# GpSimd's side work in smaller pieces: a re-spacing of the background steps of an attention and mixture-of-experts kernel

## The chip, the cores and the metric

The kernel runs on one core of one Trainium2 chip. The metric is the device time of one execution in microseconds (us), as the median of several runs. The engines are named as in the profile: PE (TensorE matmul), PEld (its weight load), DVE (VectorE), ACT (ScalarE), POOL (GpSimd), SP (SyncE, here an issuer of DMAs).

## The reference

A block of a transformer on 8 sequences of 1024 tokens with 128 features, in float32:

```
x = x + attention(layernorm(x))          # 8 heads of 16
x = x + moe(layernorm(x))                # 8 experts, the best 2 for each token
score = ((q + u) k^T + rel_shift((q + v) p^T)) / sqrt(128),  p = pos_encoding @ Wp
h = gelu(ln(x @ Wr1 + br1)) @ Wr2 + br2  # router; softmax, top 2, weights made to sum to 1
y_e = (x1 * gelu(x2)) @ W2_e + b2_e,     x1, x2 = split(x @ W1_e + b1_e)
```

The relative-position term is computed with rotation tables, so that content and position score come from products of prepared rows (`z`, `kt` and their copies) with no shift.

## The kernel before, in words

**Stages.** Attention of all eight batches comes first (about 40 to 1460 us of the profile), then the experts (to the end). Attention is cut into 32 blocks: batch b, group g of four heads, half qc of the queries (512). A block has 9 slots (`NU`), each one key tile's worth of scores, and each slot two half slots. There are thus 576 half slots of blocks, and some more until the last block has drained. In a half slot PE makes the scores for two heads of the present block (the running maximum needs them, DVE L518/L522) and the scores of an older block, 11 slots behind, again, from which ACT makes the exponentials px (L543). POOL zeroes the masked part of px (`cut`, L547, instructions L553/555/558); two slots later PE sums px times the values (`weigh`, `av` L593).

**Side work.** Everything else is written as Python generators, which run while the program is built and fix the order of each engine's instructions. `aside(h, sparing)` is called once per half slot h and lets each live generator whose time has come emit its next step; they are visited in the order of `due` (a slot number). In a generator, `yield 0` asks for PE: one such step is let out in a half slot, and in the first half of a slot only if it is due or two wait. `yield k` waits k half slots, a plain `yield` the generator's own gap (1 or 2, 3 for some). Each engine then works through its own queue in this order: an instruction that comes earlier in the program stands in front, whether it is urgent or not. The list of side generators is made by `add(slot, due, gap, make, ...)` (L1005 to 1021):

- `prepare(b)` (L345): layer norm of batch b: moments on DVE, reciprocal root on POOL (L226 to 229), the normalised xn in two POOL instructions of 128x1024 (L359, L360), the load of the next batch (SP, L362), PE's transposes xt (L370), and xall plus the output bias (POOL, L374).
- `keys(b, g)` (L381): products pq (L338), DVE's z and kt (L402), for each half of 512 the sum z + zs on POOL (L408, L409), and then sixteen copies between rows on SP's queue (L414, 415, 418, 419) to zu, ku, kl.
- `values(b)`: pv and vt, the transposed values va.
- `band`, `beside`, `close` for each block: the part of the relative position that lies outside; the division by the sum (L613 to 632, with small DMAs through `sm`, `rd`, `rx`); the sum of both groups (POOL, cx add L636); the output product `po`, added to xall (L643).
- `diagonal` (POOL L527, DVE L530): the masked maximum of the diagonal tile; `shifts` (POOL L567 to 571, PE mt L343): the maxima split in three bf16 parts.

**Routes.** After batches 1, 3, 5 and 7 a `route` is started for two batches (due: never). It normalises the rows (POOL L682, L683), multiplies by Wr1 (ph), scales (L728, L729), turns (hT, L734 to 739), applies GELU by hand on POOL and ACT (polynomial L742 to 744, tanh L772, L774, L775), multiplies by wr2h (logits, pl, L750), picks two experts, and at last scatters its rows with 32 indirect DMAs on POOL's queue (xs, L840). `table_a` and `table_b` make the tables of blocks for the experts. Never-due generators may take more steps in one half slot if these emit nothing that needs a gate:

```
more = 0 if h < 2 * (NU * 4 * NB_A) else 1 if h < 2 * total and not sparing else 3 if h >= 2 * total else 0
```

(`2*NU*4*NB_A` is 432, `2*total` is 576.) The last route works beside the experts ("late"). Experts start once the first three routes and their tables have ended and attention is past its last block.

Of the kernel before, what the change touches and what calls it, by code (L numbers as in the profile page):

```python
# [49 lines left out]
P = 128  # L50
# [98 lines left out]
def kernel(ctx: ExitStack, tc: tile.TileContext, a: dict, out: bass.AP):  # L149
# [125 lines left out]
    with ExitStack() as at:  # L275
# [69 lines left out]
        def prepare(b):  # L345

            sl = slice(b * NT, (b + 1) * NT)
            for n in range(b * NT, (b + 1) * NT):
                moments(rk, mv1, xall[:, n, :], n)
                yield  # L350

            eng = nc.gpsimd if b else nc.vector
            yield from rsqrt(eng, rk, r1[:, sl], col(mv1, 1)[:, sl], 1e-10, "p", 1.0 + 1e-5)
            xn = ap1.tile([P, NT, D], F32, name=f"xn{b}", tag="xn")
            if b == 0:
                for n in range(NT):
                    nc.vector.tensor_scalar(xn[:, n, :], xall[:, n, :], mv1[:, n, 0:1], r1[:, n:n + 1], ALU.subtract, ALU.mult)
            else:
                nc.gpsimd.tensor_tensor(xn, xall[:, sl, :], col(mv1, 0)[:, sl].unsqueeze(2).to_broadcast([P, NT, D]), ALU.subtract)  # L359
                nc.gpsimd.tensor_tensor(xn, xn, r1[:, sl].unsqueeze(2).to_broadcast([P, NT, D]), ALU.mult)  # L360
            if 0 < b < NB - 1:
                nc.sync.dma_start(xall[:, (b + 1) * NT:(b + 2) * NT, :], x_v[:, (b + 1) * NT:(b + 2) * NT, :])  # L362
            yield
            yield 2
            xts[b] = xt = ap1.tile([P, S], F32, name=f"xT{b}", tag="xT")
            for hf in range(NQ):
                yield 0
                pt = bank(f"xt{b}_{hf}") if b else scores(4 + hf)
                for n in range(TQ):
                    nc.tensor.transpose(pt[:, n * P:(n + 1) * P], xn[:, hf * TQ + n, :], ident)  # L370
                nc.scalar.activation(xt[:, hf * QB:(hf + 1) * QB], pt, AF.Identity, bias=gb[:, 1:2], scale=gb[:, 0:1])
                yield
            if b:
                nc.gpsimd.tensor_tensor(xall[:, sl, :], xall[:, sl, :], rows_bc[:, DR + NE:].unsqueeze(1).to_broadcast([P, NT, D]), ALU.add)  # L374
            yield

        def spare(name):
# [3 lines left out]
        def keys(b, g, s):  # L381

            u, xt, kl, ku, bs = f"{b}_{g}", xts[b], kls[g], kus[g], bias[g]
            tbs = []
            for hf in range(NQ):
                tb = apk.tile([P, 2, QB], F32, name=f"tb{u}_{hf}", tag="tb")
                nc.sync.dma_start(tb, a["tab"][g][:, :, hf * QB:hf * QB + QB])
                tbs.append(tb)
            yield 8
            z = apk.tile([P, S + 1], F32, name=f"z{u}", tag="z")  # L390
            zu = apk.tile([P, S], F32, name=f"zu{u}", tag="zu")
            kt = ktp.tile([P, S], F32, name=f"kt{u}", tag="kt")
            s.update(zs=(z, zu), ks=(kl, ku))
            nc.vector.memset(z[:, S:S + 1], 0.0)
            yield
            for hf in range(NQ):
                c, tb = slice(hf * QB, hf * QB + QB), tbs[hf]
                for k, t in enumerate((z, kt)):
                    yield 0
                    pq = bank(f"pq{u}_{hf}_{k}") if b + g else scores(2 * hf + k)  # L400
                    across(pq, wc[g][:, k, :], xt[:, c])
                    nc.vector.scalar_tensor_tensor(t[:, c], pq, bs[:, k:k + 1], tb[:, k, :], ALU.add, ALU.mult)  # L402
                    yield
                if b + g == 0:
                    nc.vector.scalar_tensor_tensor(z[:, c], kt[:, c], halfs[:, 1:2], z[:, c], ALU.mult, ALU.add)
                    continue
                zs = spare(f"zs{u}_{hf}")
                nc.gpsimd.tensor_scalar(zs, kt[:, c], halfs[:, 1:2], None, ALU.mult)  # L408
                nc.gpsimd.tensor_tensor(z[:, c], z[:, c], zs, ALU.add)  # L409

            q2 = nc.sync if b + g else nc.scalar
            for j in range(HG):
                r, e = 32 * j, 32 * j + DH
                nc.sync.dma_start(kl[r:e, 0:S], kt[r:e, :])  # L414
                q2.dma_start(zu[r:e, :], z[r:e, 0:S])
            for j in range(HG):
                r, e = 32 * j, 32 * j + DH
                nc.sync.dma_start(zu[e:r + 32, :], z[e:r + 32, 1:S + 1])
                q2.dma_start(ku[r:e, :], kt[r:e, :])
            yield  # L420
# [193 lines left out]
        def close(n):  # L614
# [18 lines left out]
            if g < NG - 1:  # L633
                cxs[b, qc] = cx
                return
            nc.gpsimd.tensor_tensor(cx, cx, cxs.pop((b, qc)), ALU.add)  # L636
            yield 4
            yield 0
# [20 lines left out]
        def route(t0, late):  # L659
# [16 lines left out]
            eng = nc.vector if late else nc.gpsimd  # L676
            yield from rsqrt(eng, rk, r2, col(mv2, 1)[:, sl], 1e-5)

            def rows(q):
                qs = slice(t0 + q[0], t0 + q[-1] + 1)  # L680
                xn = rw[:, q[0]:q[-1] + 1, 0:D]
                nc.gpsimd.tensor_tensor(xn, xall[:, qs, :], col(mv2, 0)[:, qs].unsqueeze(2).to_broadcast(w), ALU.subtract)  # L682
                nc.gpsimd.tensor_tensor(xn, xn, r2[:, q[0]:q[-1] + 1].unsqueeze(2).to_broadcast(w), ALU.mult)  # L683

            hs = small("hs", [nt, DR], u)
            mvh = small("mvh", [nt, 2], u)
# [20 lines left out]
            for i in range(n_q + 2):  # L707
                for k in range(4):
                    if k == 0 and i < n_q:
                        yield 0  # L710
                        turned(quads[i])
                        if i + 2 < n_q:
                            rows(quads[i + 2])
                    if k == 2 and 1 <= i <= n_q:
                        yield 0
                        narrowed(quads[i - 1])
                    if i >= 2:
                        n = quads[i - 2][k]
                        moments(rk2, mvh, hs[:, n, :], n)
                    if k % 2 == 0 or i >= 2:  # L720
                        yield
# [9 lines left out]
            def turned2(q):  # L731
                pt = bank(f"ht{u}_{q[0]}")[0:DR, :]
                for i, n in enumerate(q):
                    nc.tensor.transpose(pt[:, i * P:(i + 1) * P], hs[:, n, :], ident)  # L734
                hTs[q] = hT = rk2.tile([DR, QB], F32, name=f"hT{u}_{q[0]}", tag="hT")
                if late:
                    nc.scalar.activation(hT, pt, AF.Gelu_apprx_tanh, bias=lns[:, 1:2], scale=lns[:, 0:1])
                    return
                nc.scalar.activation(hT, pt, AF.Identity, bias=lns[:, 1:2], scale=lns[:, 0:1])

                ths[q] = th = rk.tile([DR, QB], F32, name=f"th{u}_{q[0]}", tag="th")
                nc.gpsimd.tensor_tensor(th, hT, hT, ALU.mult)  # L742
                nc.gpsimd.tensor_scalar(th, th, 0.044715, 1.0, ALU.mult, ALU.add)
                nc.gpsimd.tensor_tensor(th, th, hT, ALU.mult)

            def logits(q):
                pl = bank(f"pl{u}_{q[0]}")[:, 0:TQ * NE].rearrange("p (n k) -> p n k", k=NE)
# [9 lines left out]
            for i in range(n_q + 1):  # L757
                if i < n_q:
                    yield 0
                    if i + 2 < n_q:  # L760
                        scaled(quads[i + 2])
                    turned2(quads[i])
                yield
                if i > 0:
                    yield 0
                    logits(quads[i - 1])
                yield
                if i < n_q and not late:
                    yield
                    q = quads[i]  # L770
                    th = ths.pop(q)
                    nc.scalar.activation(th, th, AF.Tanh, scale=0.7978845608028654)  # L772
                    yield
                    nc.gpsimd.tensor_scalar(th, th, 1.0, None, ALU.add)  # L774
                    nc.gpsimd.tensor_tensor(hTs[q], th, hTs[q], ALU.mult)  # L775
                    yield


            def over(t):
# [229 lines left out]
        for m, (b, g) in enumerate(groups):  # L1009
            state[b, g] = {}  # L1010
            t0 = 2 * NU * m
            if m > 0:
                if g == 0:
                    add(t0 - 3 * NU + 2, t0 - 9, 1, prepare, b)
                add(t0 - NU - 1, t0 - 2 * NU, 1, keys, b, g, state[b, g])
            if g == 0:
                add(max(t0 - NU + 7, 0), t0 + 6, 1, values, b)
        for n in range(len(blocks_)):
            t0 = NU * n
            add(t0 + 2, t0 + 6, 3, band, n)  # L1020
# [52 lines left out]
        with tc.manual_schedule():  # L1073
# [56 lines left out]
            for t in range(last):  # L1130
# [4 lines left out]
                for half in range(2):  # L1135
# [27 lines left out]
                    if ua and a_units[ua[1]][0] == "dia":  # L1163

                        for i, (j, p) in enumerate(zip(ja, pa_)):
                            up = ap5.tile([P, QB], F32, name=f"up{ua[0]}_{j}", tag="up")
                            between.append(lambda p=p, up=up: nc.scalar.copy(up, p))
                            live.append(dict(due=t + 6, next=2 * t + half + i % 2, gap=1, gate=False,
                                             steps=diagonal(ua[0], j, up.rearrange("p (t c) -> p t c", c=P))))
                    elif ua:  # L1170
                        greatest(*ua, ja, pa_)
# [256 lines left out]
```

## Time and profile before

| what | us |
|---|---|
| median of 3 runs | 1891.94 (1890.9 to 1891.97) |
| the profiled execution | 1936.66 |
| its span, first to last instruction | 1934.8 |
| mean granted TensorE clock in it | 0.961 |
| PE, DVE, POOL, ACT busy | 1801.1, 1211.9, 1018.0, 971.0 |
| first expert matmul h (L1234) | at 1461.45 |

The page gives, beside the busy time of each engine, the span in 40 slices of 48.4 us (a digit is a tenth; PEclk is the granted clock in tenths), the chain that ended last, and groups of instructions by line. The trace can be asked for the waits of one engine ("engine line tile, what it waited for, total, times, longest"), the busy time by windows, and every instruction in order of time. A mark [8.47 <-POOL hT L775] says that the engine stood for 8.47 us before this instruction and what ended that.

Attention takes 74% of the span. In the part behind it (1461 to 1935) PE multiplies the experts' matrices.

### The profile page before, as it was taken

How to read it: one execution, taken by the hardware profiler on the slowest of the kernel's cores; microseconds unless marked ns; L12 is line 12 of the kernel's file. 1: busy time of each engine (PE TensorE's matmuls, PEld its weight loads, DVE VectorE, ACT ScalarE, POOL GpSimd, SP SyncE). 2: the span in 40 equal slices, each digit the busy share in tenths (PEclk: the TensorE clock that was granted, in tenths of full speed). 3: DMA queues.
4: the chain of work that ended last, by engine and by line, in shares of the span. 5: the costliest groups of instructions: out<-in, count | busy, mean ns of one | idle time of the engine just before them, and what ended most of it. 6: DMA issues, size and time to landing. Idle time of an engine off the chain costs nothing. (4 is left out here: it accounts for less than half of the span.)

```text
span 1934.8 us, 44523 instructions
## 1 busy us (share of the span) xinstructions
PE 1801.1 (93%) x16906; PEld 992.3 (51%) x16906; DVE 1211.9 (63%) x3203; ACT 971.0 (50%) x1851; POOL 1018.0 (53%) x1414
## 2 busy tenths in 40 slices
PE   6999999999998999899899999998989998789995
PEld 2344444444443444445344434444436887678885
DVE  5667676687685766677757566767624555444454
ACT  1265655656655555556555546655544443234442
POOL 2154363456448557763774775484752434543354
PEclk8699999999998999999989999999989999899998
DMA  5021010210102011211101120101114455455596
GB/s 153 1 59 26 27 37 28 50 35 29 26 27 37 27 36 53 58 35 30 37 26 28 54 41 27 27 27 26 32 48 142 161 170 179 142 172 188 193 322 195
DMA packets 97287, 145.65 MB, mean 75 GB/s; under 512 B 25345, under 2 KB 68610, under 8 KB 97074
## 3 DMA queue, kind: packets, MB, share of 16 engines
q1 hardware_dynamic: 78448, 117.65, 21.9%
q0 software_dynamic: 8912, 18.15, 2.6%
q10 hardware_dynamic: 9714, 7.02, 1.2%
q8 instruction: 133, 2.18, 0.5%
q14 instruction: 80, 0.66, 0.1%
HBM read 102.17 MB, written 23.55 MB: 65 GB/s over the span
## 5 line engine op out<-in xcount | busy, mean ns | idle before, releaser
L543 ACT ACTIVATE px<-sc 128x512 f32<-128x512 f32 x1152 | 632.9, 597 | 541.5 <-PE sc L507 316.8
L522 DVE CUSTOM_DVE_ANT_0 jk<-sc,wide 128x512 f32<-128x512 f32 x576 | 396.8, 689 | 156.2 <-PE sc L507 112.4
L507 PE MATMUL sc<-kl,z 32*128 32x512 f32 (+3 forms) x1536 | 404.3, 551 | 18.4 <-ACT px L543 12.1
L507 PE MATMUL sc<-ku,zu 32*128 32x128 f32 (+3 forms) x2304 | 376.9, 408 | 12.4 <-ACT px L543 8.5
L518 DVE TENSOR_REDUCE mx<-sc 128x1 f32<-128x512 f32 x448 | 287.8, 684 | 142.4 <-PE sc L507 123.0
L507 PE MATMUL sc<-zu,ku 32*128 32x512 f32 (+3 forms) x1536 | 360.1, 546 | 0.0
L593 PE MATMUL av<-px,va 128*32 128x256 f32 (+3 forms) x3792 | 351.3, 442 | 6.3 <-POOL px L555 6.2
L507 PE MATMUL sc<-z,kl 32*128 32x512 f32 (+3 forms) x1536 | 339.2, 520 | 0.2 <-ACT px L543 0.2
L1263 POOL DMA_INDIRECT ys<-yo,to x142 | 137.1, 966 | 230.6 <-DVE to L1259 79.3
L507 PEld LDWEIGHTS sc<-ku,zu 32*128 32x128 f32 x2304 | 200.6, 191 | 76.0 <-ACT px L543 53.1
L1238 DVE SCALAR_TENSOR_TENSOR gt<-h,wb,gl 128x256 f32<-128x256 f32 x280 | 135.4, 484 | 165.6 <-ACT gl L1237 125.6
L1237 ACT ACTIVATE gl<-h,wb 128x256 f32<-128x256 f32 x280 | 132.2, 473 | 169.3 <-PE h L1235 120.2
L507 PEld LDWEIGHTS sc<-kl,z 32*128 32x128 f32 x1536 | 142.5, 188 | 141.1 <-ACT px L543 100.9
L1234 PE MATMUL h<-xt,wb 128*128 128x256 f32 x560 | 174.0, 393 | 26.8 <-ACT yb L1247 10.4
L593 PEld LDWEIGHTS av<-px,va 128*32 128x32 f32 x3792 | 75.3, 108 | 231.9 <-issue 148.6
L1235 PE MATMUL h<-xt,wb 128*128 128x256 f32 x560 | 171.7, 389 | 0.0
L555 POOL TENSOR_SCALAR_AFFINE_SELECT px<-px 128x516 f32<-128x516 f32 (+1 forms) x128 | 84.8, 663 | 161.4 <-ACT px L543 161.2
L536 PE MATMUL sc<-mT,onesb 32*128 32x512 bf16 x1152 | 166.9, 382 | 2.9 <-ACT mT L578 2.8
L507 PEld LDWEIGHTS sc<-z,kl 32*128 32x128 f32 x1536 | 125.2, 186 | 67.8 <-ACT px L543 28.5
L507 PEld LDWEIGHTS sc<-zu,ku 32*128 32x128 f32 x1536 | 117.8, 186 | 80.2 <-issue 38.2
L840 POOL DMA_INDIRECT xs<-rw,slot x128 | 125.3, 979 | 32.4 <-issue 30.2
L1245 PE MATMUL y<-gt,wb 128*128 128x256 f32 x560 | 133.0, 380 | 0.3 <-ACT yb L1247 0.3
(285 smaller groups left out, 2322.0 us busy)
## 6 DMA issues: line engine op xcount, KB each, us to landing
wb<-in_wx SPq DMA_DIRECT2D x70, 772.5 KB
tb<-in_tab SPq DMA_DIRECT2D x32, 512.0 KB
xb<-xs SPq DMA_DIRECT2D x68, 130.0 KB
yk<-ys SPq DMA_DIRECT2D x32, 256.0 KB
zu<-z SPq DMA_DIRECT2D x124, 64.0 KB
xall<-in_inputs SPq DMA_DIRECT2D x8, 512.0 KB
kl<-kt SPq DMA_DIRECT2D x64, 64.0 KB
rx<-inv SPq DMA_DIRECT2D x128, 32.0 KB
```

The source lines that it names most:

```text
L507: nc.tensor.matmul(ps[:, c0:c0 + w], lhsT=lhs[r, l0:l0 + P], rhs=rhs[r, r0:r0 + w], start=first, stop=final)
L518: nc.vector.tensor_reduce(to, p, AX.X, ALU.max)
L522: nc.vector.tensor_tensor_reduce(jk, p, wide[:, m0:m0 + QB], 1.0, 3.0 * BIG, ALU.add, ALU.max, to)
L536: nc.tensor.matmul(p, lhsT=onesb[r, :], rhs=mts[n][r, :], start=first, stop=not first)
L543: nc.scalar.activation(pxs[n, k][:, j, :], p, AF.Exp)
L593: nc.tensor.matmul(avs[n][32 * j:32 * j + 32, c0:c1], lhsT=va[:, kt, j].rearrange("p o d -> p (o d)"), rhs=px[:, j, c0:c1], start=(k == 0) ...
L1234: nc.tensor.matmul(ph[:, 1, :], lhsT=wb[:, FF + c * P:FF + (c + 1) * P], rhs=xt, start=True, stop=True)
L1235: nc.tensor.matmul(ph[:, 0, :], lhsT=wb[:, c * P:(c + 1) * P], rhs=xt, start=True, stop=True)
L1237: nc.scalar.activation(gl, ph[:, 1, :], AF.Gelu_apprx_tanh, bias=wb[:, B1_0 + NFC + c:B1_0 + NFC + c + 1])
L1238: nc.vector.scalar_tensor_tensor(gt[:, c, :], ph[:, 0, :], wb[:, B1_0 + c:B1_0 + c + 1], gl, ALU.add, ALU.mult)
L1245: nc.tensor.matmul(y, lhsT=wb[:, W2_0 + c * D:W2_0 + (c + 1) * D], rhs=gt[:, c, :], start=(c == 0), stop=(c == NFC - 1))
L1263: ins = nc.gpsimd.indirect_dma_start(ys_v[HB * i + k], bass.IndirectOffsetOnAxis(ap=to[:, k:k + 1], axis=0), yo[:, k, :], None).ins
```

## The change

All edits are of the order and the size of side work; what is computed stays as it is:

```diff
# prepare (b > 0): xn in 4 instructions of 128x512 for 2 of 128x1024, a place after each
+                for n in range(0, NT, TQ):
+                    part, to = slice(b * NT + n, b * NT + n + TQ), xn[:, n:n + TQ, :]
+                    nc.gpsimd.tensor_tensor(to, xall[:, part, :], col(mv1, 0)..., ALU.subtract)
+                    yield
+                    nc.gpsimd.tensor_tensor(to, to, r1[:, part]..., ALU.mult)
+                    yield
# prepare: xall plus bias in 2 instructions of 128x512, a place after each
+                for n in range(b * NT, (b + 1) * NT, TQ):
+                    nc.gpsimd.tensor_tensor(xall[:, n:n + TQ, :], ..., ALU.add)
+                    yield
# keys: a place between zs and z + zs
                 nc.gpsimd.tensor_scalar(zs, kt[:, c], halfs[:, 1:2], None, ALU.mult)
+                yield
                 nc.gpsimd.tensor_tensor(z[:, c], z[:, c], zs, ALU.add)
# close (second group): a place before the sum of both groups
+            yield
             nc.gpsimd.tensor_tensor(cx, cx, cxs.pop((b, qc)), ALU.add)
# route: the two row instructions of a quad at two visits (k = 0, k = 1)
-                        if i + 2 < n_q:
-                            rows(quads[i + 2])
+                    if k < 2 and i + 2 < n_q:
+                        rows(quads[i + 2], k)
# route: the GELU of a quad (not late)
-                yield
                 if i < n_q and not late:
+                    q = quads[i]
+                    th, hT = ths.pop(q), hTs[q]
+                    nc.gpsimd.tensor_tensor(th, hT, hT, ALU.mult)
                     yield
-                    q = quads[i]
-                    th = ths.pop(q)
+                    nc.gpsimd.tensor_scalar(th, th, 0.044715, 1.0, ALU.mult, ALU.add)
+                    nc.gpsimd.tensor_tensor(th, th, hT, ALU.mult)
+                    yield 3
                     nc.scalar.activation(th, th, AF.Tanh, scale=0.7978845608028654)
                     yield
                     nc.gpsimd.tensor_scalar(th, th, 1.0, None, ALU.add)
-                    nc.gpsimd.tensor_tensor(hTs[q], th, hTs[q], ALU.mult)
                     yield
+                    nc.gpsimd.tensor_tensor(hT, th, hT, ALU.mult)
+                yield
# the list of side work
-                    add(t0 - 3 * NU + 2, t0 - 9, 1, prepare, b)
+                    add(t0 - 3 * NU + 2, t0 - 2 * NU + 2, 1, prepare, b)
-                add(max(t0 - NU + 7, 0), t0 + 6, 1, values, b)
+                add(max(t0 - NU + 7, 1), t0 + 6, 1 if b else 3, values, b)
# the diagonal's due
-                            live.append(dict(due=t + 6, ...steps=diagonal(...)))
+                            live.append(dict(due=t + 2, ...steps=diagonal(...)))
```

The polynomial stood in `turned2` (L742 to 744) before; its three lines are removed there. POOL gets three instructions more for each of seven batches. On PE, `weigh` sums a px in two column halves only where no gated step waits (`split`), so the number of av instructions shifts slightly with the order.

More of the change, by code (lines that the diff above doesn't have):

```diff
@@ L358, in prepare @@
             else:
-                nc.gpsimd.tensor_tensor(xn, xall[:, sl, :], col(mv1, 0)[:, sl].unsqueeze(2).to_broadcast([P, NT, D]), ALU.subtract)
-                nc.gpsimd.tensor_tensor(xn, xn, r1[:, sl].unsqueeze(2).to_broadcast([P, NT, D]), ALU.mult)
+                for n in range(0, NT, TQ):
+                    part, to = slice(b * NT + n, b * NT + n + TQ), xn[:, n:n + TQ, :]
+                    nc.gpsimd.tensor_tensor(to, xall[:, part, :], col(mv1, 0)[:, part].unsqueeze(2).to_broadcast([P, TQ, D]), ALU.subtract)
+                    yield
+                    nc.gpsimd.tensor_tensor(to, to, r1[:, part].unsqueeze(2).to_broadcast([P, TQ, D]), ALU.mult)
+                    yield
             if 0 < b < NB - 1:
@@ L373, in prepare @@
             if b:
-                nc.gpsimd.tensor_tensor(xall[:, sl, :], xall[:, sl, :], rows_bc[:, DR + NE:].unsqueeze(1).to_broadcast([P, NT, D]), ALU.add)
+                for n in range(b * NT, (b + 1) * NT, TQ):
+                    nc.gpsimd.tensor_tensor(xall[:, n:n + TQ, :], xall[:, n:n + TQ, :], rows_bc[:, DR + NE:].unsqueeze(1).to_broadcast([P, TQ, D]), ALU.add)
+                    yield
             yield
@@ L677, in route, with rows @@
             yield from rsqrt(eng, rk, r2, col(mv2, 1)[:, sl], 1e-5)
-            def rows(q):
+            def rows(q, part=2):
                 qs = slice(t0 + q[0], t0 + q[-1] + 1)
                 xn = rw[:, q[0]:q[-1] + 1, 0:D]
-                nc.gpsimd.tensor_tensor(xn, xall[:, qs, :], col(mv2, 0)[:, qs].unsqueeze(2).to_broadcast(w), ALU.subtract)
-                nc.gpsimd.tensor_tensor(xn, xn, r2[:, q[0]:q[-1] + 1].unsqueeze(2).to_broadcast(w), ALU.mult)
+                if part != 1:
+                    nc.gpsimd.tensor_tensor(xn, xall[:, qs, :], col(mv2, 0)[:, qs].unsqueeze(2).to_broadcast(w), ALU.subtract)
+                if part != 0:
+                    nc.gpsimd.tensor_tensor(xn, xn, r2[:, q[0]:q[-1] + 1].unsqueeze(2).to_broadcast(w), ALU.mult)
             hs = small("hs", [nt, DR], u)
@@ L741, in turned2 @@
                 ths[q] = th = rk.tile([DR, QB], F32, name=f"th{u}_{q[0]}", tag="th")
-                nc.gpsimd.tensor_tensor(th, hT, hT, ALU.mult)
-                nc.gpsimd.tensor_scalar(th, th, 0.044715, 1.0, ALU.mult, ALU.add)
-                nc.gpsimd.tensor_tensor(th, th, hT, ALU.mult)
             def logits(q):
@@ L1167 @@
                             between.append(lambda p=p, up=up: nc.scalar.copy(up, p))
-                            live.append(dict(due=t + 6, next=2 * t + half + i % 2, gap=1, gate=False,
+                            live.append(dict(due=t + 2, next=2 * t + half + i % 2, gap=1, gate=False,
                                              steps=diagonal(ua[0], j, up.rearrange("p (t c) -> p t c", c=P))))
```

## The prediction

> **What bounds the kernel now.** I first read the page's sections 1 and 2 (busy time, slices, granted clock).
>
> ```profile
> PE 1801.1 (93%) x16906; PEld 992.3 (51%) x16906; DVE 1211.9 (63%) x3203; ACT 971.0 (50%) x1851; POOL 1018.0 (53%) x1414
> ...
> PE   6999999999998999899899999998989998789995
> ...
> PEclk8699999999998999999989999999989999899998
> ```
>
> TensorE is the bound: 93% busy, the next engine 63%. GpSimd (POOL) has nearly half its time free, so it can cost time only by being late at a place where PE waits. PE and PEclk both dip near slices 13, 15 and 20: PE stands, then runs slower. The list of what PE waited for, over attention's steady part (120 to 1415 us), gives names:
>
> ```profile
> PE pl L750 <- POOL hT L775: 22.3, 4, 8.5
> PE sc L507 <- ACT px L543: 20.0, 55, 2.0
> PE sc L507 <- issue: 4.6, 4, 3.0
> PE pq L338 <- DVE kt L402: 3.1, 1, 3.1
> ```
>
> (total us, times, longest.) The largest is one hand-over: the router's logits wait for hT from POOL, two of the four waits 8.5 us. To price a disturbance I cut the trace into windows of two blocks (36 half slots), so that like is compared with like:
>
> ```profile
> 193.00:274.40 81.40, 80.33 (x920) 36.80 (x912) 59.99 (x153) 47.26 (x91) 36.70 (x62) 1.00 0.17 37
> ...
> 517.40:601.10 83.70, 81.72 (x1019) 38.95 (x1012) 64.96 (x187) 48.87 (x93) 43.46 (x76) 1.00 0.17 37
> 601.10:698.50 97.40, 88.07 (x934) 41.80 (x930) 61.70 (x164) 52.58 (x98) 61.81 (x81) 0.93 0.13 26
> 698.50:788.10 89.60, 84.67 (x916) 38.40 (x912) 60.04 (x153) 47.08 (x90) 61.72 (x83) 0.98 0.22 54
> ...
> 1056.80:1153.90 97.10, 87.48 (x917) 40.24 (x912) 60.08 (x153) 47.50 (x90) 68.36 (x97) 0.93 0.19 48
> ```
>
> (window, length, busy us and count of PE, PEld, DVE, ACT, POOL, then granted clock, DMA share, GB/s.) An undisturbed pair of blocks takes 80 to 84 us. The pairs in which a route and its scatters run take 88 to 97. Summed over all fifteen windows of 113 to 1413 us, what exceeds the quiet ones is about 90 us: that is what a better order on POOL can win at most. The order of time on POOL shows how the first one arises:
>
> ```profile
> 605.76 1.90 POOL L359 TENSOR_TENSOR xn<-xall,mv 128x1024 f32<-128x1024 f32 x1
> 607.74 1.90 POOL L360 TENSOR_TENSOR xn<-xn,r 128x1024 f32<-128x1024 f32 x1
> 609.60 1.50 POOL L774 TENSOR_SCALAR th<-th 64x512 f32<-64x512 f32 x1
> 611.18 1.25 POOL L775 TENSOR_TENSOR hT<-th,hT 64x512 f32<-64x512 f32 x1
> ```
>
> and the matching rows of PE and of a window:
>
> ```profile
> 612.49 1.87 PE L750 MATMUL pl<-wr2h,hT 64*128 64x8 f32 x8 [8.47 <-POOL hT L775]
> ```
>
> ```profile
> 604.00:620.00 16.00, 7.53 (x56) 3.73 (x52) 2.54 (x8) 2.02 (x4) 13.20 (x17) 0.57 0.00 0
> ```
>
> From 595.5 POOL never rests: GELU polynomial, two reciprocal roots, masks, shifts, the two long xn, then hT. By half slot 252 of the program it is 14 us behind the other engines. logits is emitted one half slot behind hT, so PE takes the whole lag.
>
> **The change, part by part.** Durations are of the profiled execution (1936.66 us, span 1934.8, 1.86 around it); its ratio to the median of the runs, 1891.94, is 0.977, and I multiply the sum by that. "h" counts half slots (some 2.3 us each, 576 in attention).
>
> *Route spread (polynomial off L742–744, tanh three half slots later, th·h apart, logits two half slots behind it; rows() over two visits).* Nothing is added to any engine; each POOL op keeps its time (1.03, 0.61, 1.27, 1.49, 1.26). I kept account of POOL's queue in the order of the changed program, by the rows' durations: on the old order it reproduces the old lag within about 1 us. On the new one the lag at h249–253 is 8 to 10 us instead of 14, and logits comes two half slots later, so its wait vanishes. What is late next is the tanh on ScalarE (queued behind it: the exps px, which PE needs): about 2.2 us at each place. What one event costs now: 8.47 of wait, then the half clock. The granted clock falls at 606.1 and returns at 619.8, 7.3 us after PE resumed, so 3.65 us are lost after the wait. "TensorE: Matmul & The Clock Gate" of the Trainium skill (Part 1) says that about 3.4 us of sustained work bring back full clock; that would make 1.7 us. The row decides: 8.47+3.65 = 12.1, near the window's excess over quiet, 97.4−83.8 = 13.6. Less 2.2 of new wait and 0.9 for its effect, −10.5. The window from 959.4 is the same again (97.4): −10.5.
>
> *xn in 4 pieces of 128x512, x+bias in 2, with yields.* Nearest row for a half: rw L682/683, 1045 and 1040 ns, against 1901/2 and 1895/2: +0.19 each, and 2357 becomes about 2×1275. Per batch 0.56 us, ×7 = 3.9 us of POOL, which is 53% busy: nothing while the lag is below what the consumers leave. With the earlier due, xn no longer waits behind scatters: PE's gaps of 5.7 us at 792–801 (among them 1.5 for xt on xn) go: −5 in 788–875. prepare ends some 4 half slots later (h259 to h263 for the first); keys starts at a fixed slot, and that still suffices. The load of the next batch (L362) moves with xn in SP's queue, a batch ahead of need: 0.
>
> *Diagonal due t+2 (first among its fellows).* It takes 4×0.65 us of POOL ahead of others; 0, within ±2 in all.
>
> *Scatters.* A route now ends 10 to 20 half slots later (h287 to 301, 431 to 441, 551 to 571), so its 32 scatters (0.97 each, 1.27 apart in a burst) fall elsewhere: h304–339 for 290–325; h443–467 for 433–457; h573–586 for 553–576. First set: the lag at h320–331 falls from 14 to about 7: half of that window's excess of 8 over 81.5, −4. Second set: the old pile in 1056.8–1153.9 (standstills of 3.0 at 1077, the pq wait of 3.1, the half clock behind) leaves it, −12, and a new one comes in the next window: by the account stalls of 1.1 at h456 and 3.2+0.8+2.1+1.75 at h468–472, 9 us, with the clock +12. 1237–1325 and 1325–1413: the logits' waits of 1.4 and 4.0 go, with part of the clock behind: −3, −4.
> Third set: from h576 four scatters may go per half slot, and now 30 of the 32 do. 30×1.27 = 38 us on POOL, plus masks and shifts about 9: 47 us for 11 half slots of 2.3. Block 31's masks stand behind them, and av waits for these. Before, attention ended 49.5 us after h575 (1412 to 1461.5), with an av wait of 3.6 behind four scatters. I get 58 to 61.5: +9 to +12; I take +12, since the clock falls there.
>
> *keys: a place between zs and z add.* The 16 copies on SP are issued after it.
>
> ```profile
> 258.88 1.27 POOL L409 TENSOR_TENSOR z<-z,zs 128x512 f32<-128x512 f32 x1
> ```
>
> ```profile
> 270.31 0.59 SPq L419 DMA_DIRECT2D ku<-kt  x1
> ```
>
> z add ends at 260.15, the issues run at 0.63 each to 270.9, the last lands about 12 us after the add, and the next block's first use of heads 2, 3 is at 279.06: slack about 7 us. The z add comes two half slots (4.6 us) and a mask or two later, about 6 us. So slack falls to 0–1 us at some 8 tight starts of the 15. Ends: 0, or 3.5 us at each if POOL is further behind (38, below). The nearest row says 6 of 7 used: I take +5.
>
> *close: a place before cx add.* po two half slots later; po only starts the route later. 0.
>
> *Opening: values in every third half slot.* In 40–98 the clock is half to 87.3 and DVE sets the slots; moving pv (1.9 us each at half clock) between them: −2 (ends −6 and +4).
>
> Sum: −10.5−10.5−4−5−12+12−3−4+12+5−2 = −22 us of 1936.66; ×0.977 = −21.5, so **1870 us**.
>
> **Rivals.**
> *More is won* (13%): the tail's scatters hide in the half slots, as earlier ones did in bursts of four, and new piles cost no clock: 0 for the tail and half of +12 for the second set, −40, 1853. For it: POOL has 47% free. Against: the tail of before already shows 3.6 behind four scatters.
> *Tail pile* (12%): POOL sets attention's end, and the masks of block 31 plus the fetch of the experts' rows wait for the last scatter: +25 in place of +12, and the clock: −8, about 1884 (1880 to 1893).
> *Slower by the keys* (20%): the z add comes 10 us later, not 6, because masks, diagonal (now first) and xn pieces stand before it; slack is 7, so every start of a group waits. It decides at about 9 us, where some 24 us are lost: 8 starts ×3.5 and 7 ×1.5 = 38 with the clock, −27+38 = +11: about 1903. For it: zs and its add were one step, and each yield lets others in. Against: POOL's lag near the keys was small (the add at 258.88 began at once).
> *Nothing* (5%): the wait moves from logits to tanh and so to px, with equal length: 1892. Against: the new order's lag is 4 to 6 us lower.
>
> **How the numbers follow.** A measurement here can tell about 0.2%, 3.8 us. Forecast 50% (1858 to 1884), more 13%, tail pile 12% (7 faster, 5 same), keys 20%, nothing 5%. Faster 70%, same 10%, slower 20%. The range 1848 to 1903 leaves out the outer half of the keys' case and the best of "more"; the likeliest case's own range is 1858 to 1884.
>
> **What would show it.** Right: no logits wait on hT; 601–698 and 959–1057 near 86 with clock 1.00; a longer tail after h575 with av waiting for px; scatters beside the keys in the window after 1154. Wrong: ku or zu landing after first use, with PE waiting on DMA at block starts; a second wait, tanh, of more than 3 us; a tail no longer than 50 us.

## The result, and the profile after

The changed kernel takes 1920.13 us (median of 4 runs, 1918.89 to 1922.92) beside 1891.95 for the kernel before: a ratio of 1.0149, interval [1.0134, 1.0165]. It is 28 us slower; the prediction was 22 us faster.

The kernel before takes 1891 to 1892 us in some sets of runs (the "lower level"; a set is made on one chip) and 1937 to 1942 in others (the "upper level"), and the profile on which the prediction was made, 1936.66, lies at the upper level, while the runs of before and the profile of after lie at the lower. The right partner for the changed kernel is therefore a second profile of the unchanged one (the run b0, span 1890.8); ratios are always made within a set.

The page of the changed kernel, sections 1 and 2:

```profile
PE 1780.1 (93%) x16778; PEld 973.6 (51%) x16778; DVE 1226.5 (64%) x3203; ACT 972.8 (51%) x1851; POOL 1020.1 (53%) x1435
...
PE   6999999999999999999999989999968998799995
...
PEclk8699999999999999999999989999989999899998
```

The dips of the page before near slices 13 and 20 are gone. Others stand at slices 24, 30 and 35 (47.9 us each): the second set of scatters, the end of attention (the "tail"), and a place among the experts. These three are most of this result.

Then what PE waited for, from 40 to 1500 us (total, times, longest), in the changed kernel:

```profile
PE sc L514 <- ACT px L550: 24.1, 65, 1.0
PE av L600 <- POOL px L562: 18.4, 9, 5.2
PE av L600 <- POOL px L565: 8.0, 1, 8.0
...
PE pl L757 <- POOL hT L786: 5.2, 3, 2.2
```

The wait of the logits fell from 22.3 us (22.4 in b0) to 5.2; the forecast was that it would vanish. In its place stands av, which waits 26.4 us for POOL's masks of px (6.6 in b0). No copy of the keys (zu, ku, kl) is in the list.

Next, windows cut at the same half slots in both. An "event" is a stretch in which the logits waited: half slots 238 to 256, 382 to 400 and 526 to 544. The rows are: first event; second event; second set of scatters, half slots 436 to 472; third event; the tail, half slot 562 to the first expert product; the experts. The kernel before at the lower level (b0):

```profile
568.10:622.20 54.10, 44.50 (x484) 20.73 (x480) 33.32 (x92) 25.96 (x48) 39.75 (x59) 0.91 0.17 33
...
918.40:973.20 54.80, 45.13 (x484) 20.82 (x480) 33.69 (x92) 26.02 (x49) 39.83 (x59) 0.91 0.18 33
1058.30:1139.90 81.60, 79.99 (x912) 36.57 (x908) 61.05 (x157) 46.71 (x88) 70.40 (x97) 1.00 0.23 56
1264.40:1316.20 51.80, 45.79 (x488) 21.98 (x484) 31.94 (x80) 26.04 (x50) 36.83 (x44) 0.93 0.15 24
...
1356.20:1439.20 83.00, 74.83 (x668) 29.75 (x668) 27.91 (x73) 45.56 (x83) 48.94 (x65) 0.90 0.15 48
1439.20:1890.80 451.60, 419.14 (x2140) 362.70 (x2140) 237.10 (x660) 177.47 (x367) 204.21 (x215) 0.97 0.60 198
```

and the changed kernel (a second profile of it, after_again, span 1916.4):

```profile
573.10:617.50 44.40, 41.12 (x460) 17.83 (x456) 33.94 (x91) 24.29 (x46) 32.18 (x59) 1.00 0.21 41
...
917.70:962.00 44.30, 41.03 (x460) 17.82 (x456) 33.84 (x91) 24.24 (x45) 32.08 (x58) 1.00 0.21 41
1052.00:1145.90 93.90, 82.97 (x926) 36.77 (x922) 62.21 (x169) 46.22 (x87) 70.14 (x99) 0.95 0.20 50
1271.50:1313.70 42.20, 41.65 (x472) 18.97 (x468) 30.50 (x73) 25.45 (x47) 33.09 (x42) 1.00 0.18 30
...
1359.30:1452.70 93.40, 73.26 (x679) 30.37 (x671) 35.26 (x97) 45.36 (x83) 55.69 (x74) 0.87 0.16 48
1452.70:1916.40 463.70, 419.11 (x2140) 362.61 (x2140) 239.54 (x662) 177.61 (x367) 203.99 (x215) 0.97 0.58 193
```

The three events become 9.7, 10.5 and 9.6 us shorter and their clock is 1.00 again. The second set of scatters becomes 12.3 longer, the tail 10.4, and the experts, of which the prediction spoke only in passing, 12.1, with the same 2140 products and the same busy PE (419.1): it is all waiting.

The whole account, after_again less b0, stretch by stretch from the starts and ends of these windows and what lies between:

| stretch | us |
|---|---|
| up to the first event (573.1 − 568.1) | +5.0 |
| first event, and the stretch behind it | −9.7 + 4.7 |
| first set of scatters, and the stretch behind it | −1.8 + 1.1 |
| second event, and the stretch behind it | −10.5 + 4.9 |
| second set of scatters, and the stretch behind it | +12.3 + 1.1 |
| third event, and the stretch behind it | −9.6 + 5.6 |
| tail (to the first expert product) | +10.4 |
| experts | +12.1 |
| sum (1916.4 − 1890.8) | +25.6 |

One stretch alone is not certain to its last us: the other profile of the same changed kernel (after, span 1917.2) has 86.8 us behind the first event and 129.2 at the first scatters, where after_again has 89.9 and 124.5. The three long rows (second scatters, tail, experts) agree within 0.2.

### The profile page after: what moved, and what is told of

It reads as the page before. It is cut to its first block, busy times and chain, and to the rows that moved or that the text cites. A ratio compares the mean times of both kernels' runs of the same rounds, so it can differ in the third digit from the quotient of the medians.

```text
span 1917.2 us, 44241 instructions
## 1 busy us (share of the span) xinstructions
PE 1780.1 (93%) x16778; PEld 973.6 (51%) x16778; DVE 1226.5 (64%) x3203; ACT 972.8 (51%) x1851; POOL 1020.1 (53%) x1435
## 3 DMA queue, kind: packets, MB, share of 16 engines
q1 hardware_dynamic: 78448, 117.65, 22.4%
## 5 line engine op out<-in xcount | busy, mean ns | idle before, releaser
L529 DVE CUSTOM_DVE_ANT_0 jk<-sc,wide 128x512 f32<-128x512 f32 x576 | 396.9, 689 | 126.3 <-PE sc L514 82.0
L514 PE MATMUL sc<-ku,zu 32*128 32x128 f32 (+3 forms) x2304 | 367.8, 402 | 8.4 <-ACT px L550 5.9
L514 PEld LDWEIGHTS sc<-ku,zu 32*128 32x128 f32 x2304 | 195.4, 188 | 67.4 <-ACT px L550 50.0
L1245 PE MATMUL h<-xt,wb 128*128 128x256 f32 x560 | 170.0, 386 | 23.3 <-issue 16.3
L1246 PE MATMUL h<-xt,wb 128*128 128x256 f32 x560 | 167.7, 381 | 0.0
L543 PE MATMUL sc<-mT,onesb 32*128 32x512 bf16 x1152 | 162.0, 381 | 0.0
L534 POOL TENSOR_SCALAR_AFFINE_SELECT up<-up 128x512 f32<-128x512 f32 x128 | 81.0, 637 | 107.2 <-ACT up L1178 107.0
```

Of the source, the lines that this page charges most:

```text
L514: nc.tensor.matmul(ps[:, c0:c0 + w], lhsT=lhs[r, l0:l0 + P], rhs=rhs[r, r0:r0 + w], start=first, stop=final)
L529: nc.vector.tensor_tensor_reduce(jk, p, wide[:, m0:m0 + QB], 1.0, 3.0 * BIG, ALU.add, ALU.max, to)
L543: nc.tensor.matmul(p, lhsT=onesb[r, :], rhs=mts[n][r, :], start=first, stop=not first)
L1245: nc.tensor.matmul(ph[:, 1, :], lhsT=wb[:, FF + c * P:FF + (c + 1) * P], rhs=xt, start=True, stop=True)
L1246: nc.tensor.matmul(ph[:, 0, :], lhsT=wb[:, c * P:(c + 1) * P], rhs=xt, start=True, stop=True)
```

## The experiments

**The kernel before again (b0).** No edit.

> The kernel before, unchanged, for a second profile: the profiled execution took 1936.66 us, 45 more than the median of its runs, while the changed kernel's profiled execution (1918.89) agrees with its median (1920.13). Theory A (the two long waits of the logits for hT and the half clock behind each are not in most executions): the new profile spans about 1890 us, and the windows around 601 to 698 and 959 to 1057 take about 84 to 86 us instead of 97. Theory B (the difference lies in the experts' part): attention again ends near 1460 us and the experts take about 430 us instead of 473. Theory C (that one execution was slow throughout): every window is 2.3% shorter.

Measured: 1892.36 us, ratio 1.0005 [0.9997, 1.0012]. None of the three theories holds as put. Theory A is wrong: both waits of 8.5 us are there. Of the 44 us between the two profiles of one kernel, 22 lie in attention and 22 among the experts. In attention the largest part (14.5 us) is at half slots 436 to 472, which take 81.6 us here and 96.1 there. So the pile at the second set of scatters, from which the prediction took −12 us, does not exist at the lower level.

**One line alone, and all but one line.** Four kernels in one set (upper level, kernel before 1941.59).

```diff
# close_only: before, with this line; all_but_close: after, without it
+            yield
             nc.gpsimd.tensor_tensor(cx, cx, cxs.pop((b, qc)), ALU.add)
# gelu_only: before, with the router's GELU as in the change
# all_but_diagonal: after, with
-        live.append(dict(due=t + 2, ...
+        live.append(dict(due=t + 6, ...
```

> The kernel before with one line of the change: the place in close ahead of the sum of both groups. Read from the profiles: attention of the changed kernel ends 14 us later than in a typical execution of the kernel before (experts' first product at 1452 against 1438), and its experts' part is 12 us longer (465 against 453). Theory 1 (the loss is made at the end: the last route and the tables, late by this place, meet the experts and the tail worse): experts +12, the tail +3 to +8 as the third set of scatters moves from half slots 553-576 to 561-579; 1904 to 1912 us. Theory 2 (the keys' copies come late, the rival of the prediction): this line touches no key, 1892. Theory 3 (the diagonal, now first, holds VectorE up): 1892.

Measured: 1951.79, ratio 1.0048 [1.0037, 1.006], +10 us, just under the 12 to 20 of theory 1. The parts are as theory 1 said: the experts take 485.9 us (473.3 in the profile of before), the tail 86.4 (79.8). The experts' rows of before and of close_only:

```profile
1461.50:1934.80 473.30, 426.73 (x2140) 367.94 (x2140) 236.72 (x660) 176.70 (x367) 203.60 (x215) 0.96 0.57 189
...
1463.90:1949.80 485.90, 428.70 (x2140) 369.06 (x2140) 239.24 (x662) 176.72 (x367) 204.01 (x215) 0.94 0.55 184
```

The line acts in attention too: the first two events fall from 55 to 44 us, and the stretches behind them rise from 86 to 95. In the first of these av waits 6.0 us in one piece for a mask: most of the wait moved to another step behind POOL.

> The changed kernel without the place in close. The order of the experts' side work is then that of the kernel before, and the third set of scatters lies at half slots 567-583 in place of 573-586. Theory 1: the experts' part back to 453 us (-12) and the tail shorter by 4 to 8: 1900 to 1905. Theory 2 and theory 3: still 1918 to 1920.

Measured: 1941.34, 1.0002 [0.9989, 1.0015]. The experts are back at 473.4. The tail is not shorter, 94.4: that part of the expectation failed, so in the changed kernel the tail does not come from close. The total is not told apart from the changed kernel's at this level (1.0014 in after_third, below); close is seen here in the experts alone.

> The kernel before with only the router's GELU spread over more places. The waits of the logits at three places (8.5, 8.5, and 1.4 with 4.0) go with the half clock behind them: -28 in attention as in the profile of the changed kernel (9.7, 9.0, 9.6). Theory 1: the route is 12 half slots longer, the third set of scatters lies at 567-583, so the tail gives 5 to 10 back, and the second set (441-465, beside the keys) 3 to 8: 1872 to 1880. Theory 2: nothing is lost at the keys, which are as before: 1864. Theory 3: 1864 too.

Measured: 1924.4, 0.9908 [0.9888, 0.9928], −17 us. The events shrink by 11, 11 and 9; the tail is 94.9 (79.8 before) and half slots 436 to 472 take 98.5 (96.1). So the spread GELU alone brings the gain at the events and also the tail's loss, as theory 1 said.

> The changed kernel with the diagonal's due at t+6 again. Theory 3 (its waits, sc after mx on VectorE 7.6 us in all and about 1 us in each pair of quiet blocks, are the diagonal's): -8 to -12, 1908 to 1912. Theory 1 and theory 2: 1918 to 1920.

Measured: 1948.73, 1.0045 [1.0028, 1.0061]. Theory 3 falls: nothing is gained, and the stretch to the first event, 577.7 us, is no shorter than the changed kernel's (573.1).

**Controls, iotas, and the time of prepare.** Four kernels in one set (lower level, kernel before 1891.82).

> The changed kernel, unchanged, for a control beside the others: in the last four runs the kernel before itself took 1941.6 us and its profile showed waits of VectorE for nothing the trace shows (25 us among the experts) and standstills in bursts of scatters, while in the run of b0 it took 1891.4 and showed none. So there are two levels of the kernel before, and the prediction was made on a profile of the slower. If the level comes with the chip: where the kernel before takes about 1892, this takes 1920 (ratio 1.015); where it takes 1941, the profile-based sum leaves -22 plus the 12 of the experts and 5 to 10 elsewhere, 1.000 to 1.007 of it.

Measured: 1919.64, 1.0148 [1.0131, 1.0165]: as it said.

```diff
# after_iota: after; in table_b the iotas of own, inrow and unused stand ahead of this line
             eb, kb, _ = yield from blocks_of(NB2, nb.rearrange("p a e -> p (a e)"), "b")
# prepare_later: before, with
-                    add(t0 - 3 * NU + 2, t0 - 9, 1, prepare, b)
+                    add(t0 - 3 * NU + 7, t0 - 9, 1, prepare, b)
# prepare_later_logits: prepare_later, with (not late) logits(quads[i - 1]) behind th times h of quad i
```

> The changed kernel, with three iotas of table_b (own, inrow, unused, on GpSimd) placed ahead of blocks_of instead of behind it; no step or place is added. Theory 1a: the experts' 12 us come mostly from one meeting: the place in close moves the last route so that its second labels (GpSimd, waiting 3.3 us for the landing of the first sixteen scatters) stand right ahead of the iotas, VectorE's next step waits 7 to 9 us for them, and the experts' gt and xt stand behind it. Then the experts fall by 8 to 10 us and the wait of hsown vanishes; ratio to the changed kernel 0.995. Theory 1b (the experts' loss is that the last route as a whole is late, whatever meets): no change.

Measured: 1909.6, 1.009 [1.0074, 1.0107], −10 us against the changed kernel. This is theory 1a: the experts take 453.1 us, PE's "issue" waits before h fall from 16.4 to 6.8, and the wait of hsown is gone.

```profile
1454.50:1907.60 453.10, 417.72 (x2140) 361.56 (x2140) 239.39 (x662) 177.22 (x367) 203.69 (x215) 0.98 0.60 197
```

What went is seen on three engines of the changed kernel (after_again). On POOL, in order of time:

```profile
1652.30 0.96 POOL L851 DMA_INDIRECT xs<-rw,slot  x1 [0.30 <-issue]
1656.61 0.21 POOL L847 COPY rw<-m 128x16 f32<-128x16 f32 x1 [3.35 <-DMA xs<-rw,slot]
1656.75 0.21 POOL L848 COPY rw<-dsts 128x16 int32<-128x16 int32 x1
1656.90 0.66 POOL L966 IOTA hsown<- 128x480 f32 x1
```

On DVE:

```profile
1657.60 0.66 DVE L971 TENSOR_TENSOR hsown<-ebb,hsown 128x480 f32<-128x480 f32 x1 [9.43 <-POOL hsown L966]
1658.17 0.48 DVE L1249 SCALAR_TENSOR_TENSOR gt<-h,wb,gl 128x256 f32<-128x256 f32 x1
...
1660.09 0.41 DVE L1235 COPY xt<-xp 128x256 f32<-128x256 f32 x1
```

On PE:

```profile
1660.61 1.19 PE L1245 MATMUL h<-xt,wb 128*128 128x256 f32 x2 [9.79 <-issue]
```

The second labels (rw, L847 and L848) wait for the first scatters to have landed, the iota stands behind them, a cheap step of table_b on DVE stands 9.43 us for the iota, and behind that stand gt and xt of the next experts' block. PE stops for 9.8 us before its next h. In b0 the same wait of DVE (L960 for L955) is 2.0. The trace names this wait of PE "issue"; only DVE's queue tells what it was.

> The kernel before with one number changed: prepare is started five slots (ten half slots) later, nothing cut up. Theory 4 (the two waits of 8.5 us are the meeting of xn with the router's GELU on GpSimd, not the size of the pieces or the closeness of the places): the events near half slots 252 and 396 shrink by 6 to 10 us each while the scatters stay where they are (291-326, 435-459, 553-576) and the tail and the experts stay as before: -12 to -20, ratio 0.990 to 0.994. If only the spreading of the GELU helps: 1.000.

Measured: 1870.46, 0.9882 [0.9865, 0.9898], −21 us: a little more than expected. The events take 46.3 and 47.9 us (54.1 and 54.8), half slots 292 to 346 119.9 (126.3), and tail and experts are as in b0 (82.9, 451.9). PE's waits for hT, 22.4 us in b0 with two of 8.5, are now:

```profile
PE pl L750 <- POOL hT L775: 9.4, 4, 4.0
```

Nothing was cut up. The two large waits were a meeting of xn with the router's GELU.

> The same, and logits of a quad one visit later (behind th times h of the next quad), with the polynomial and tanh where they were. The route is 3 or 4 half slots longer in place of 12. The third event (near half slot 530) goes too, -9: ratio 0.985 to 0.990; the third set of scatters at 557-578 costs the tail at most 3 us.

Measured: 1868.99, 0.9878 [0.9862, 0.9895]. The third event goes (44.1 for half slots 526 to 544, 51.8 in b0), but the windows that end at half slots 418, 526 and 562 give most of it back (3.3, 2.5 and 2.0 us more than in prepare_later). This kernel has the lowest median of all, and is not told apart from prepare_later.

**The second set, the tail, the keys and the pieces.** Four kernels in one set (upper level, before 1941.75).

```diff
# after_prepare_later: after, with
-                    add(t0 - 3 * NU + 2, t0 - 2 * NU + 2, 1, prepare, b)
+                    add(t0 - 3 * NU + 6, t0 - 2 * NU + 2, 1, prepare, b)
# third_route_close: after; GELU in its old places where t0 == 2 * NRT
# keys_only: before, with a yield between zs and z + zs
# pieces_only: before, with prepare as in the change (pieces and due)
```

> The changed kernel with prepare started four slots (eight half slots) later. Theory 4 (a meeting on GpSimd is what costs, wherever the scatters or the GELU of a route fall together with the normalising of prepare): in the changed kernel the second set of scatters (half slots 443-467) meets prepare of the last batch, which starts at 454 (windows 436-454 and 454-472 together 94 us against 81.5 in the kernel before). With prepare from 462 on, its xn come after the scatters: -8 to -12, ratio to the kernel before 1.009 where the changed kernel has 1.015. If the scatters alone make the pile: no change.

Measured: 1942.36, 1.0013 [0.9996, 1.0029]. Without the changed kernel in the same set this shows neither a gain nor its absence.

> The changed kernel with the GELU of the third route alone in its old places. Its scatters then lie at 561-579 in place of 573-586. If the tail's +10 (93 against 83 us from half slot 562 to the experts) is made by scatters let out four in a half slot ahead of the last block's masks: the tail falls to about 86, as in close_only; in return the wait of the logits near half slot 530 is back, +9 in the window 526-544. Sum: -2 to +4 against the changed kernel. If the tail is made by something else: tail 93, and +9.

Measured: 1939.84, 1.0002 [0.999, 1.0014]. The tail is 86.4, as forecast: the place of the third route's scatters makes most of its loss. The event came back by 2.4 us only (44.6). The total is still that of the changed kernel (1.0014 in after_third), since the experts take 485.2 us where they take 478.2 there; no run tells why.

> The kernel before with only the place between zs and its sum in keys. The prediction put +5 on it, and its rival up to +38 with PE waiting at block starts. By the changed kernel's trace the last copy lands about 11 us after the sum and the first use of it comes later than that in all fifteen groups, and PE never waits for a copy: so 0 to +4 (first route's scatters 294-329, second 437-461): ratio 0.999 to 1.002. The rival: 1.01 or more.

Measured: 1938.1, 0.9985 [0.9972, 0.9998]. The rival of the prediction falls. The first two events shrink even here (55 to 46.7 each), but the stretches behind them grow by 6.7 and 3.9: as in close_only, most of the wait moved on to other steps behind POOL.

> The kernel before with only prepare cut up (four and two pieces with places) and its earlier due. If the size of the pieces is what makes GpSimd late, the events near half slots 252 and 396 shrink here as they did with the GELU spread (-10 each): ratio 0.990. Theory 4: the xn still meet the GELU of the route, only four half slots further apart; part of it, -2 to -8 in all: 0.996 to 0.999.

Measured: 1930.81, 0.9948 [0.9938, 0.9958], −11 us. The first two events shrink by 3 to 4 each, not by the 10 of the sizes, and the total lies between the two forecasts (0.990, and 0.996 to 0.999). The run holds two edits, the pieces and the earlier due, and does not tell them apart.

**Both mends, with partners.** The changed kernel beside after_prepare_later, and that with the iotas moved; first at the upper level (before 1936.87), then again at the lower (before 1891.06).

> The changed kernel again, as the partner of the next run on the same chip. Where the kernel before takes about 1892: 1920 (1.015). Where it takes 1941, if close_only (1.005), all_but_close (1.000) and all_but_diagonal (1.0045) add up: 1.003 to 1.008, so that the change loses less there.

Measured: 1940.37, 1.0014 [1.0003, 1.0025]. At the upper level the change costs 3 us, not 28: there the kernel before already has a pile at the second set, and the changed kernel takes 96.7 us where that takes 96.1; the experts are 4.9 us longer, not 12.1.

> The changed kernel with prepare four slots later, again, beside it. In its profile PE's waits for masks at the second set of scatters fell from 8.7 us (av 7.5, mt 1.2) to 1.7, with the half clock behind them. Theory 4: 8 to 12 us less than the changed kernel in the same call. If what went there comes back elsewhere: less than 4.

Measured: 1936.45, 0.9997 [0.9983, 1.0011], 4 us less than its partner; theory 4 had 8 to 12, and "less than 4" stood for a gain that comes back elsewhere.

> Both mends on the changed kernel: prepare four slots later, and the three iotas of table_b ahead of blocks_of. If the two costs are independent, their gains add: 8 to 12 and 10, so 18 to 22 us less than the changed kernel in the same call; about 1900 where the kernel before takes 1892, which leaves the tail's 10 us.

Measured: 1935.0, 0.9997 [0.9985, 1.0008], 5 us less than the changed kernel. The two gains don't add up here.

> The changed kernel with prepare four slots later, a third time. Beside a kernel before of about 1937 to 1942 it came to 1.0013 and 0.9997 (the changed kernel 1.0014), which does not show the 8 to 12 us. If the kernel before takes about 1892 in this call, theory 4 gives 1.009 where the changed kernel has 1.0148 and the windows 436-472 fall from 94 to 84 us; if the gain comes back elsewhere, 1.013 or more. Otherwise 0.9997 to 1.0013 again.

Measured: 1917.82, 1.0147 [1.0131, 1.0164]: 2 us less than the changed kernel's 1919.64 (1.0148) of the earlier set, no more than the sets differ. That is the second case of the expectation, a gain that comes back elsewhere. The window of the second set:

```profile
1050.50:1139.00 88.50, 79.96 (x926) 35.66 (x922) 62.73 (x169) 46.16 (x86) 65.56 (x86) 1.00 0.22 53
```

Its waits from 1060 to 1150 us, in after_again and here:

```profile
PE av L600 <- POOL px L562: 7.5, 4, 3.4
...
PE av L600 <- POOL px L562: 4.5, 4, 1.8
```

The window falls from 93.9 to 88.5 us, and av's wait from 7.5 to 4.5, so some 5 of the 12 us go with the time of prepare; what makes the other 7 is not shown. The experts are 2.7 us longer again, and the stretch up to the first event 5.3.

> Both mends again: 1.003 to 1.005 where the kernel before takes about 1892 and the gains add (the iotas alone gave 1.009), 1.008 if only the iotas count; otherwise 0.9997 again.

Measured: 1905.94, 1.0084 [1.0067, 1.0101]: the iotas count (1.009 with them alone); what prepare adds, 0.0006 of the ratio or 1 us, is not told apart from nothing.

## Why the prediction was wrong

**What bounds the kernel** was read rightly, and so were the three waits of the logits: −10.5, −10.5 and (−3−4) were put down, −9.7, −10.5 and −9.6 measured. But each is followed by a stretch that is about 5 us longer in after_again (1.6, 1.7 and 5.6 in the profile of after): in each the logits, now later, wait for hT again, 2.3, 2.3 and 2.1 us. The agreement at the events is partly luck. The −10.5 was already net: 13.6 us of excess, less 3.1 for new waits. Measured are 9.7 at the first event and 4.7 handed on, so the gain was put too high and what comes back too low. Net, the three are worth 14.6 us in after_again, not 28.

**A term put at nothing: "close: a place before cx add. po two half slots later; po only starts the route later. 0."** It measured +12 us among the experts. The last route works beside them; shifted, its second labels meet table_b's iotas on POOL. close_only shows the 12 us with this line alone, all_but_close shows the experts without them, and after_iota shows that 10 of the 12 are this one meeting. The prediction saw that the route starts later and did not ask what it would then meet.

**The term of the old pile, "−12", failed because of its base.** It was taken from a profile at the upper level, where half slots 436 to 472 take 96.1 us. At the lower level, that of the median, they take 81.6 (b0). The new pile, "+12", measured +12.3 on that quiet base, and at the half slots that were forecast (PE's waits of about 1 us and more, at half slots 456 to 470, add up to 8.8 us; 9 were put down): that half was right, and it is a loss and not an exchange. Scaling by 0.977 could not mend this, since the difference of the levels is not spread evenly. The sign was there and was only scaled away: the profiled execution was 45 us longer than every run.

**The tail, "+9 to +12, I take +12"**, measured +10.4, by the mechanism named: in after_again 30 of the 32 scatters start after half slot 576 (7 in b0), and av waits for the masks. The waits in the tail, of b0 and of after_again:

```profile
PE av L593 <- POOL px L555: 2.9, 3, 1.3
...
PE av L600 <- POOL px L562: 8.6, 2, 5.2
PE av L600 <- POOL px L565: 8.0, 1, 8.0
```

third_route_close takes 6 to 7 us of the loss away (86.4; after_third 92.1, after_again 93.4).

**First scatters −4 and xn −5**: −0.7 together with the stretch behind in after_again, +3.5 in the profile of after. PE's waits for POOL at the first scatters are only 4.4 us in b0, and 1.8 in after_again: there was little to gain.

**Keys +5, opening −2**: the stretch up to the first event is 5 us longer. keys alone is no loss: keys_only is no slower than the kernel before (0.9985). It reaches half slot 238 3.0 us later, and its PE waited there for px (8.2 us in 25 waits, 100 to 560 us; 5.8 in 20 in b0), never for a copy. Which edit makes the other 2 us is not shown; the opening was not tried alone. The rival ("slower by the keys", 1903) gave the right sign from the wrong cause.

**Pieces**: their price was put at 3.9 us of POOL, and by the durations it is 3.8 (14 each of 1.041, 1.040 and 1.268 us for 7 each of 1.901, 1.895 and 2.357). pieces_only is 11 us faster, so the price does not show in the time; whether the gain is the pieces' or the earlier due's is open.

**The sum.** From −22 to the +25.6 of the stretches are 47.6 us: 13.4 are the three events with what they handed on, 12 the old pile that was not there, 12.1 close, 8.3 the first scatters and xn, and the rest 2 or less each. No single term explains the miss; the sign is decided by several together.

Two small readings do not hold, and no term rests on them: the page of before dips in PE at slice 17, not 15, and the opening's clock was full from 42.9 to 53.1 us, so half from 53.1 to 87.3 and not from 40.

What stays open: what makes the two levels. In each of the twelve profiles at the upper level DVE's gt has waits on "issue" among the experts, 16 to 40 us in all (39.5 in the prediction's profile), and in none of the eight at the lower. Three sets lie at each level, each on another chip; no run tells whether the chip makes the level. Also open are the other 7 us at the second set.

## What to carry to other kernels

Before a prediction is built on a profile, its own time must be near the runs' median; if it is not, take each term from a stretch that both show, or call it unknown. When side work of several origins shares an in-order queue, look for the two that meet and move one start; here one number (the start of prepare) gained 21 us, and all the cutting and spreading together lost 28, both at the lower level. Whatever lengthens a chain of background steps also moves everything behind it: follow the chain to the end of the kernel, into stages that the edit does not touch.

## What was not expected of the hardware

The half clock around the first stall lasted 13.65 us in the prediction's profile and 10.24 in b0, with the same wait of 8.5 us at the same place; it outlasted PE's return by 7.3 and 5.5 us. And a wait on another engine can be reported as "issue": 9.8 us of PE, with DVE standing 9.43 us behind POOL, and POOL 3.35 us behind a DMA.
